# Layer 0 of a four-layer graph kernel: y1 summed on GpSimd before its transposition, and the adjacency's diagonal fetched by strided DMAs

## The chip, the cores and the metric

The kernel runs on one core of one Trainium2 chip. The metric is the device time of one execution in microseconds; a time of several runs is their median. The core has TensorE (PE, with its weight loads shown apart as PEld), VectorE (DVE), ScalarE (ACT), GpSimd (POOL) and SyncE (SP), which here only issues DMAs. All engines run their own instruction queue in order and wait for each other by semaphores.

## The reference, cut to what matters

Four layers follow one another, each of the form `x = layernorm(x + layer(x, adj))`, with x of shape (8, 2048, 64) and adj of shape (2048, 2048). The change is in layer 0:

```python
def _L0_gnn_ref(x, A, embedding, weight, bias):
    K, N = weight.shape[1], A.shape[-2]                      # K = 3, N = 2048
    w = jnp.einsum('nd,dkio->nkio', embedding, weight)
    b = jnp.einsum('nd,do->no', embedding, bias)
    As = [jnp.eye(N, dtype=x.dtype), A]
    As.append(2.0 * (A @ As[-1]) - As[-2])
    x_g = jnp.einsum('knm,bmc->bnkc', jnp.stack(As, 0), x)
    return jnp.einsum('bnki,nkio->bno', x_g, w) + b
```

So layer 0 needs x, y1 = A x and 2 A y1 - x. The matrix A that setup_inputs makes is a 0/1 pattern with each row divided by its sum and with ones on the pattern's diagonal. Row n of A is therefore a 0/1 row times one number, and that number stands on A's diagonal. The kernel calls it s1; it computes with the 0/1 mask and scales the rows of the product by s1.

## The kernel before, in words

Data are held with 128 graph nodes on the partitions and batch and feature (8 x 64 = 512) along the free dimension; there are 16 such node tiles. fp32 values that go through the fast fp32r matmul are split into a rounded part and a remainder (x_hi and x_lo, y_hi and y_lo), and both are multiplied.

**First product** (`first_product`, lines 404 to 508). It makes y1 = s1 * (mask @ x). It runs over four quarters of 512 output nodes, and in each quarter over eight pieces (four blocks of A's transpose, two halves each), 32 pieces in all. `begin(n)`, called two pieces ahead, has SyncE load the piece of A (`raw`, line 439), has VectorE turn it into the 0/1 mask `m` (line 441) and, in the first quarter only, loads a block of x and splits it (`split_x`: load at line 414, x_hi on ScalarE at line 419, x_lo on VectorE at line 420). raw and xraw share four buffers. A piece is sixteen matmuls (line 471) into four accumulator banks, one for each output tile of the quarter; the pool has six banks, and a seventh and eighth belong to small work (`sm0`).

The diagonal is taken in the same pass. In the quarter's first two pieces VectorE multiplies the diagonal blocks with the identity (`dg`, line 451). PE sums them over the partitions by a matmul with ones (`sp`, line 483), ScalarE copies the result into a row `sb` (line 486), one piece later four single-column matmuls turn the row into columns (`sc`, line 491), and VectorE copies them into `s1` (line 495). At the quarter's end ScalarE writes `y_hi` (line 500) and VectorE `y_lo` (line 501), both scaled by s1. After the last quarter the row goes to DRAM as `s_row` (line 507), and `s2 = 2 * s1` is made on VectorE (line 508). Between the pieces runs a generator, `steps`, that prepares membership lists for layer 1 (pT, oh, S, rk; the constants tri, ltri and iota for it are made by GpSimd).

**The loop of layer 0** (`layer0`). For each of the 16 node tiles: SyncE loads two halves of A (`load_adj`, line 966) and the row of s1 for that tile, spread over the partitions (`srow`, line 972), and the x pieces (`load_x`); VectorE makes the mask (`mask`, line 986); GpSimd multiplies the mask by srow and sums its columns (`scaled`, lines 994 to 1002), and VectorE compares that with A (`compare`, line 1007). `first_terms` transposes y1 of the tile for the later matmuls: for each of four 128-column blocks two fp32r matmuls with the identity, one of y_hi and one of y_lo, which PSUM adds up (line 1017); ScalarE copies the result out as y1T (line 1022). `product` makes the second product (line 1044), `second_term` transposes it by `transpose`, a plain fp32 transpose on PE (line 154). `weigh` multiplies the three terms by the weights (line 1081), and VectorE sums them up with the embedding as factor (line 1092). The loop is written as a software pipeline: in iteration j, between the eight groups g of tile j's `weigh`, it runs `scaled(j + 1, 0)` after g = 1, `first_terms(j + 1)` after g = 2, and the product, the comparison and the masks of the next tiles after g = 3.

**What sets the order.** The engines' compute instructions inside `with program_order()` keep the order in which the code calls them, each engine for itself. All else (SyncE's DMAs, and instructions outside those blocks, s2 among them) is placed by a scheduler between them, as early as it reckons that its inputs are there. Buffers come from pools with a fixed number per tag; a tile that takes over a buffer waits for the last reader of the one before. Memory of a pool that is closed is used again by the next, so first tiles of the loop also wait for the last stores of the first product.

Of the kernel before, what the change touches and what calls it, by code (L numbers as in the profile page):

```python
# [8 lines left out]
F32 = mybir.dt.float32  # L9
# [9 lines left out]
P = 128  # L19
# [32 lines left out]
def kernel(  # L52
# [350 lines left out]

    def first_product(own, pre, rawp, mskp, y_hi, y_lo, prepare):

        sb = pre.tile([P, N], F32, tag="sb", name="sb")
        x_hi, x_lo = buffer(own, 0, "x_hi"), buffer(own, 1, "x_lo")
        with tc.tile_pool(name="acc0", bufs=6, space=PSUM) as ps_acc, tc.tile_pool(
            name="sm0", bufs=1, space=PSUM
        ) as ps_s:  # L410
            def split_x(g, h):
                raw = rawp.tile([P, 2, QW], F32, tag="raw", name=f"xraw_{g}_{h}")
                lo = g * QW + h * 2 * P
                nc.sync.dma_start(
                    raw, xn[lo:lo + 2 * P, :].rearrange("(t p) c -> p t c", p=P)
                )
                for t in range(2):
                    j = 4 * g + 2 * h + t
                    nc.scalar.copy(r_(x_hi[:, j, :]), raw[:, t, :])  # L419
                    nc.vector.tensor_tensor(  # L420
                        r_(x_lo[:, j, :]), raw[:, t, :], x_hi[:, j, :], ALU.subtract
                    )

            steps = prepare(ps_s)
            pieces = [
                (q, i, kk, h)
                for q in range(NQ)
                for i, kk in enumerate([q] + [kk for kk in range(4) if kk != q])
                for h in range(2)
            ]  # L430
            m_of, dgs, accs = {}, {}, {}

            def begin(n):

                if n >= len(pieces):
                    return
                q, i, kk, h = pieces[n]
                raw = rawp.tile([P, 2, QW], F32, tag="raw", name=f"raw_{q}_{kk}_{h}")
                nc.sync.dma_start(raw, at[q, kk][:, 2 * h:2 * h + 2, :])
                m = mskp.tile([P, 2, QW], F32, tag="m", name=f"m_{q}_{kk}_{h}")  # L440
                nc.vector.tensor_scalar(r_(m), raw, 0.0, None, op0=ALU.is_gt)
                m_of[n] = m
                if q == 0:
                    split_x(kk, h)
                if i == 0:

                    if h == 0:
                        dgs[q] = pre.tile([P, 4, P], F32, tag="dg", name=f"dg_{q}")
                    for t in range(2):
                        jj = 2 * h + t  # L450
                        nc.vector.tensor_tensor(
                            dgs[q][:, jj, :], raw[:, t, jj * P:(jj + 1) * P], ident, ALU.mult
                        )

            with program_order():
                begin(0)
                begin(1)
                for n, (q, i, kk, h) in enumerate(pieces):
                    begin(n + 2)
                    qc = slice(q * QW, (q + 1) * QW)  # L460
                    if i + h == 0:
                        accs[q] = [
                            ps_acc.tile([P, BC], F32, tag="acc", name=f"y1p_{4 * q + jj}")
                            for jj in range(4)
                        ]
                    m = m_of.pop(n)
                    for t in range(2):
                        mt = 4 * kk + 2 * h + t
                        for jj in range(4):
                            for part in (x_hi, x_lo):  # L470
                                nc.tensor.matmul(  # L471
                                    accs[q][jj],
                                    r_(m[:, t, jj * P:(jj + 1) * P]),
                                    r_(part[:, mt, :]),
                                    start=i + h + t == 0 and part is x_hi,
                                    stop=i == 3 and h + t == 2 and part is x_lo,
                                )
                        if n > 8 or (n, t) == (6, 0):
                            for _ in range(1 + t):
                                next(steps, None)  # L480
                    if (i, h) == (0, 1):
                        sp = ps_s.tile([P, QW], F32, tag="sp", name=f"sp_{q}")
                        nc.tensor.matmul(
                            sp, ones, dgs[q].rearrange("p j n -> p (j n)"), start=True, stop=True
                        )
                        nc.scalar.copy(sb[:, qc], sp)
                    if (i, h) == (1, 0):
                        sp = ps_s.tile([P, QW], F32, tag="sp", name=f"sc_{q}")
                        for jj in range(4):
                            j = 4 * q + jj  # L490
                            nc.tensor.matmul(
                                sp[:, jj:jj + 1], sb[0:1, j * P:(j + 1) * P], ones[0:1, 0:1],
                                start=True, stop=True,
                            )
                        nc.vector.tensor_copy(cols_of["s1"][:, 4 * q:4 * q + 4], sp[:, 0:4])
                    if (i, h) == (3, 1):
                        for jj in range(4):
                            j = 4 * q + jj
                            s = cols_of["s1"][:, j:j + 1]
                            nc.scalar.activation(r_(y_hi[:, j, :]), accs[q][jj], AF.Copy, scale=s)  # L500
                            nc.vector.scalar_tensor_tensor(
                                r_(y_lo[:, j, :]), accs[q][jj], s, y_hi[:, j, :],
                                op0=ALU.mult, op1=ALU.subtract,
                            )
                for _ in steps:
                    pass
            nc.sync.dma_start(s_row, sb[0:1, :])
            nc.vector.tensor_scalar(cols_of["s2"], cols_of["s1"], 2.0, None, op0=ALU.mult)

    @with_exitstack  # L510
# [428 lines left out]
    def layer0(  # L939
# [21 lines left out]
        def load_adj(j):  # L961
            raws[j] = []
            for h in range(2):
# [4 lines left out]
                        at[j // 4, 2 * h + k][:, :, (j % 4) * P:(j % 4 + 1) * P],  # L968
                    )
                raws[j].append(raw)  # L970
            srow[j] = tile("srow", f"srow_{j}", (P, P), 3)
            nc.sync.dma_start(srow[j], s_row[0, j * P:(j + 1) * P].partition_broadcast(P))

        def load_x(j):
# [37 lines left out]
        def first_terms(j):  # L1012

            tr = ps_tr.tile([P, NP, P], F32, tag="tr", name=f"try1_{j}")
            for pr in range(NP):
                for part in (y_hi, y_lo):
                    nc.tensor.matmul(  # L1017
                        tr[:, pr, :], r_(part[:, j, pr * P:(pr + 1) * P]), r_(ident_r),
                        start=part is y_hi, stop=part is y_lo,
                    )  # L1020
            y1T = tile("y1T", f"y1T_{j}", (P, NP, P))
# [1061 lines left out]
```

## Time and profile before

| | |
|---|---|
| median of 3 runs | 1359.8 us (1359.33 to 1364.57) |
| profiled execution | 1364.6 us |
| its span, first to last instruction | 1362.9 us |
| PE busy | 1304.4 us, 96% |
| VectorE busy | 919.2 us, 67% |
| GpSimd busy | 420.2 us, 31% |
| ScalarE busy | 370.7 us, 27% |
| mean granted PE clock | 0.96 |
| first PE matmul | 7.1 us |
| end of the first product's matmuls | 148.7 us |
| layer 0's loop | about 153 to 715 us |

[...]

This is not to be read as PE at its peak, as a matmul counts as busy while it is in the pipeline; PE's time is better read from where its instructions start. "Idle before, releaser" in the other views names the event that ended an engine's waiting. The chain of waits goes back from the last instruction to what released it, again and again; a share in it is time that the end of the span depended on.

### The profile page before, as it was taken

The numbers are of one execution on the slowest core, as the hardware profiler recorded it, in microseconds if no ns is written. First come the engines' busy times: TensorE is split into PE (matmuls) and PEld (weight loads), VectorE is DVE, ScalarE is ACT, GpSimd is POOL, SyncE is SP. The second block draws the span as 40 slices with busy tenths as digits, with TensorE's granted clock in tenths as the row PEclk, the third lists the DMA queues.
The fourth block names the chain that finished last, engine by engine and source line by source line (L and its number), as shares of the span: only waits on it lengthen the run. The fifth ranks groups of instructions, "written<-read, shape, count | busy, mean of one in ns | idle before, by whom it ended". The sixth has DMA issues, their size and how long they took to land.

```text
span 1362.9 us, 20154 instructions
## 1 busy us (share of the span) xinstructions
PE 1304.4 (96%) x7884; PEld 1019.4 (75%) x7884; DVE 919.2 (67%) x1611; ACT 370.7 (27%) x844; POOL 420.2 (31%) x353
## 2 busy tenths in 40 slices
PE   7999899999999999999986799999998899999997
PEld 6777688888888888888874466666665788888885
DVE  4555378787777777777663768888885656666454
ACT  3000101121112222222221345666665521111111
POOL 0000353444444444444210445666553510000000
PEclk9999899999999999999985788999998899999999
DMA  8865432333333333331604111222220223334552
GB/s 285 238 187 167 135 111 89 104 103 103 103 103 103 103 103 104 104 101 55 232 24 140 69 52 65 77 78 78 78 78 1 93 94 124 115 109 141 185 185 72
DMA packets 91047, 153.01 MB, mean 112 GB/s; under 512 B 12097, under 2 KB 55489, under 8 KB 84673
## 3 DMA queue, kind: packets, MB, share of 16 engines
q1 hardware_dynamic: 88642, 147.46, 32.4%
q10 hardware_dynamic: 2304, 4.20, 0.8%
q8 instruction: 64, 1.05, 0.3%
q14 instruction: 37, 0.30, 0.1%
HBM read 115.97 MB, written 35.66 MB: 111 GB/s over the span
## 4 chain that ended last, share of the span: by engine, by line
PE 92%; DVE 3%; ACT 2%; DMA 1%; issue 1%; POOL 0%; SPq 0%; ACTq 0%; DVEq 0%; POOLq 0%
PE pp L1081 25%; PE a L1353 17%; PE ind L1353 9%; PE y2p L1044 9%; PE y1p L471 9%; PE fc L801 3%; PE df L810 2%; PE gp L696 2%; PE trm L154 1%; PE yp L1441 1%; PE try L1017 1%; PE aggp L1190 1%; PE dp L721 1%; PE sgp L1138 1%; PE red L746 1%; PE u L866 1%
## 5 line engine op out<-in xcount | busy, mean ns | idle before, releaser
L1092 DVE SCALAR_TENSOR_TENSOR r<-pp,emb_sb,r 128x256 f32<-128x256 f32 x512 | 247.4, 483 | 123.5 <-PE pp L1081 109.8
L1081 PE MATMUL pp<-w_sb,xT 64*128 64x256 f32 x1024 | 160.4, 390 | 1.7 <-DVE r L1092 1.7
L1081 PE MATMUL pp<-w_sb,y1T 64*128 64x256 f32 x1024 | 153.5, 376 | 0.0
L1081 PE MATMUL pp<-w_sb,y2T 64*128 64x256 f32 x1024 | 153.5, 376 | 0.0
L1030 POOL TENSOR_TENSOR r<-xs,bn 128x256 f32<-128x256 f32 x32 | 22.6, 727 | 413.7 <-issue 263.0
L471 PE MATMUL y1p<-x_hi,m 128*128 128x512 f32 x256 | 106.7, 417 | 7.2 <-ACT x_hi L419 7.1
L1081 PEld LDWEIGHTS pp<-w_sb,xT 64*128 64x128 f32 x1024 | 94.4, 186 | 25.1 <-issue 14.9
L737 POOL TENSOR_TENSOR ez<-ez,coef 128x1024 f32<-128x1024 f32 x32 | 65.1, 2033 | 142.2 <-DVE ez L735 119.8
L1081 PEld LDWEIGHTS pp<-w_sb,y1T 64*128 64x128 f32 x1024 | 99.7, 187 | 10.9
L1081 PEld LDWEIGHTS pp<-w_sb,y2T 64*128 64x128 f32 x1024 | 99.6, 187 | 11.0
L1353 PE MATMUL ind<-y_hi,mj_l 128*128 128x512 f32 x256 | 106.2, 415 | 0.8 <-DVE dlt L766 0.7
L1044 PE MATMUL y2p<-y_hi,msk 128*128 128x512 f32 x256 | 103.7, 405 | 0.0
L471 PE MATMUL y1p<-x_lo,m 128*128 128x512 f32 x256 | 101.9, 398 | 0.0
L1353 PE MATMUL a<-y_hi,mj_l 128*128 128x512 f32 x256 | 101.3, 396 | 0.6 <-ACT y_hi L874 0.6
L1044 PE MATMUL y2p<-y_lo,msk 128*128 128x512 f32 x256 | 101.7, 397 | 0.0
L1353 PE MATMUL a<-y_lo,mj_l 128*128 128x512 f32 x256 | 101.2, 395 | 0.0
L1353 PE MATMUL ind<-y_lo,mj_l 128*128 128x512 f32 x256 | 100.9, 394 | 0.0
L1353 PE MATMUL a<-v_hi,mj_l 128*128 128x512 f32 x256 | 100.1, 392 | 0.0
L1353 PE MATMUL a<-v_lo,mj_l 128*128 128x512 f32 x256 | 99.9, 391 | 0.0
L994 POOL TENSOR_TENSOR ms<-msk,srow 128x1024 f32<-128x1024 f32 x32 | 89.9, 2811 | 5.7 <-DVE ms L1007 5.7
L1353 PEld LDWEIGHTS ind<-y_hi,mj_l 128*128 128x128 f32 x256 | 48.5, 190 | 33.7 <-issue 18.1
L986 DVE TENSOR_SCALAR msk<-adj 128x1024 fp32r<-128x1024 f32 x32 | 63.7, 2024 | 4.1 <-PE y1p L471 4.1
(269 smaller groups left out, 2413.6 us busy)
## 6 DMA issues: line engine op xcount, KB each, us to landing
mj_l<-mask SPq DMA_DIRECT2D x48, 1024.0 KB, 4.9
raw<-in_at SPq DMA_DIRECT2D x32, 512.0 KB, 5.1
adj<-in_at SPq DMA_DIRECT2D x64, 256.0 KB, 3.6
mask<-msk SPq DMA_DIRECT2D x32, 512.0 KB, 4.5
xraw<-in_xn SPq DMA_DIRECT2D x8, 512.0 KB, 5.6
oh<-oh SPq DMA_DIRECT2D x16, 256.0 KB, 3.7
xT<-in_xt SPq DMA_DIRECT2D x16, 256.0 KB, 2.9
xs<-in_xn SPq DMA_DIRECT2D x16, 256.0 KB, 2.8
```

What stands on the lines that cost most here:

```text
L471: nc.tensor.matmul(accs[q][jj], r_(m[:, t, jj * P:(jj + 1) * P]), r_(part[:, mt, :]), start=i + h + t == 0 and part is x_hi, stop=i == 3 a ...
L696: nc.tensor.matmul(gp[:, u, :], r_((oh01, oh23)[i][rs, cols]), r_(part[rs]), start=part is agg_hi, stop=part is agg_lo,)
L737: nc.gpsimd.tensor_tensor(by_b(ez), by_b(ez), per_b(coef, 2 * i, 2), ALU.mult)
L801: nc.tensor.matmul(fc[:, h, :], fcw_sb[rs], sT[rs], start=True, stop=True)
L810: nc.tensor.matmul(df[:, b:b + 1], th[:, b % 2, (b // 2) * P:(b // 2 + 1) * P], av_sb, start=True, stop=True,)
L986: nc.vector.tensor_scalar(r_(m), raws[j][h], 0.0, None, op0=ALU.is_gt)
L994: nc.gpsimd.tensor_tensor(ms, m, srow[j].unsqueeze(1).to_broadcast([P, 8, P]), ALU.mult)
L1030: nc.gpsimd.tensor_tensor(r[:, 4 * bq * C:4 * (bq + 1) * C] .rearrange("p (h l c) -> p h l c", h=2, l=2), swapped(terms[j]["xs"], bq), bn. ...
L1044: nc.tensor.matmul(acc, r_(msk[j, mt // 8][:, mt % 8, :]), r_(part[:, mt, :]), start=mt == 0 and part is y_hi, stop=mt == NT - 1 and part ...
L1081: nc.tensor.matmul(pp[:, h, pl, :], terms[j][name][rs, 2 * bq + pl], w_sb[rs, k, dq * 4 * C:(dq + 1) * 4 * C], start=k == 0, stop=k == K - 1,)
L1092: nc.vector.scalar_tensor_tensor(rb, ppv[:, :, dd, :], emb_sb[:, j, d:d + 1], rb, op0=ALU.mult, op1=ALU.add)
L1353: nc.tensor.matmul(acc, r_(a[:, mt, :]), r_(part[:, mt, :]), start=mt == 0 and part is hi, stop=mt == NT - 1 and part is lo,)
```

## The change

There are three edits.

- In the first product dg, sp, sb, sc and their copies are gone. When piece 7 is begun, GpSimd issues four DMAs (one for each quarter, 128 partitions x 4 elements of 4 bytes, strided in DRAM along the diagonal) straight into s1, and then one DMA that writes s1 from SBUF to s_row. The accumulator pool gets a seventh bank in place of the bank that sp and sc used in turns with the lists' work: sm0 keeps its one bank for the lists.
- In the loop, tiles 2 to 15: GpSimd adds y_hi and y_lo into a tile y1 (one buffer), and PE transposes that by `transpose`, four instructions in place of eight. Tiles 0 and 1 stay as they were.
- srow has two buffers in place of three.

```diff
     def first_product(own, pre, rawp, mskp, y_hi, y_lo, prepare):
-        sb = pre.tile([P, N], F32, tag="sb", name="sb")
         x_hi, x_lo = buffer(own, 0, "x_hi"), buffer(own, 1, "x_lo")
-        with tc.tile_pool(name="acc0", bufs=6, space=PSUM) as ps_acc, tc.tile_pool(
+        with tc.tile_pool(name="acc0", bufs=7, space=PSUM) as ps_acc, tc.tile_pool(
             name="sm0", bufs=1, space=PSUM
         ) as ps_s:
...
-                if i == 0:
-
-                    if h == 0:
-                        dgs[q] = pre.tile([P, 4, P], F32, tag="dg", name=f"dg_{q}")
-                    for t in range(2):
-                        jj = 2 * h + t
-                        nc.vector.tensor_tensor(
-                            dgs[q][:, jj, :], raw[:, t, jj * P:(jj + 1) * P], ident, ALU.mult
+                if n == 7:
+
+                    for qq in range(NQ):
+                        d = at[qq, qq]
+                        nc.gpsimd.dma_start(
+                            cols_of["s1"][:, 4 * qq:4 * qq + 4],
+                            bass.AP(d.tensor, d.offset, [[4 * QW + 1, P], [QW + P, 4]]),
                         )
+                    nc.gpsimd.dma_start(
+                        s_row.rearrange("o (t p) -> p (o t)", p=P), cols_of["s1"]
+                    )
...
-                    if (i, h) == (0, 1):
-                        sp = ps_s.tile([P, QW], F32, tag="sp", name=f"sp_{q}")
-                        nc.tensor.matmul(
-                            sp, ones, dgs[q].rearrange("p j n -> p (j n)"), start=True, stop=True
-                        )
-                        nc.scalar.copy(sb[:, qc], sp)
-                    if (i, h) == (1, 0):
-                        sp = ps_s.tile([P, QW], F32, tag="sp", name=f"sc_{q}")
-                        for jj in range(4):
-                            j = 4 * q + jj
-                            nc.tensor.matmul(
-                                sp[:, jj:jj + 1], sb[0:1, j * P:(j + 1) * P], ones[0:1, 0:1],
-                                start=True, stop=True,
-                            )
-                        nc.vector.tensor_copy(cols_of["s1"][:, 4 * q:4 * q + 4], sp[:, 0:4])
...
-            nc.sync.dma_start(s_row, sb[0:1, :])
             nc.vector.tensor_scalar(cols_of["s2"], cols_of["s1"], 2.0, None, op0=ALU.mult)
...
-            srow[j] = tile("srow", f"srow_{j}", (P, P), 3)
+            srow[j] = tile("srow", f"srow_{j}", (P, P))
...
         def first_terms(j):
             tr = ps_tr.tile([P, NP, P], F32, tag="tr", name=f"try1_{j}")
+            if j > 1:
+                y1 = tile("y1", f"y1_{j}", bufs=1)
+                nc.gpsimd.tensor_tensor(y1, y_hi[:, j, :], y_lo[:, j, :], ALU.add)
             for pr in range(NP):
+                pc = slice(pr * P, (pr + 1) * P)
+                if j > 1:
+                    transpose(tr[:, pr, :], y1[:, pc])
+                    continue
+
                 for part in (y_hi, y_lo):
                     nc.tensor.matmul(
-                        tr[:, pr, :], r_(part[:, j, pr * P:(pr + 1) * P]), r_(ident_r),
+                        tr[:, pr, :], r_(part[:, j, pc]), r_(ident_r),
                         start=part is y_hi, stop=part is y_lo,
                     )
```

More of the change, by code (lines that the diff above doesn't have):

```diff
@@ L430, in first_product @@
             ]
-            m_of, dgs, accs = {}, {}, {}
+            m_of, accs = {}, {}
             def begin(n):
@@ L459, in first_product @@
                     begin(n + 2)
-                    qc = slice(q * QW, (q + 1) * QW)
                     if i + h == 0:
```

## The prediction, made before the changed kernel had run

> **What bounds the kernel now.** I read the page first (span, engines, the chain of waits), then the stretches of the two stages that the change touches, then the chain inside them, and last the time lines of VectorE, GpSimd and SyncE, and what the DMA queues moved.
>
> ```profile
> span 1362.9 us, 20154 instructions
> PE 92%; DVE 3%; ACT 2%; DMA 1%; issue 1%; POOL 0%; SPq 0%; ACTq 0%; DVEq 0%; POOLq 0%
> ```
>
> TensorE holds 92% of the chain that ended last. The stretches say whether that is so where the change is made (the columns are the time, then the busy time of PE, PEld, DVE, ACT and POOL, the granted clock, the DMA share, GB/s):
>
> ```profile
> 20.00:60.00 40.00, 40.00 (x180) 31.91 (x180) 21.87 (x48) 7.87 (x14) 0.00 (x0) 1.00 0.87 251
> 60.00:120.00 60.00, 58.78 (x249) 44.08 (x248) 34.86 (x101) 5.44 (x9) 0.00 (x0) 1.00 0.59 179
> 163.00:715.00 552.00, 547.46 (x4292) 459.92 (x4290) 419.79 (x786) 108.74 (x217) 220.66 (x202) 0.99 0.31 102
> ```
>
> PE is full from 20 us on in the first product and full in the tile loop of layer 0 (163 to 715 us); VectorE there is at 76%, GpSimd at 40%. In the first product the DMA is the runner-up: 87% of its time up to 60 us, 59% after. So a PE instruction taken out of either stage is time, unless something else comes late. The chain gives the prices:
>
> ```profile
> 17.30 0.86 PE sp L483 x2
> ...
> 21.83 0.98 PE sc L491 x8
> ...
> 49.10 1.05 PE sp L483 x2
> ...
> 54.25 0.98 PE sc L491 x8
> ```
>
> ```profile
> 271.89 1.04 PE try L1017 x8
> ...
> 292.91 0.59 PE try L154 x4
> ```
>
> The first pair are the diagonal's two visits to PE, in two of the four quarters. The second set out the two ways of transposing 128x512 in the loop: y1 today, as hi plus lo in eight matmuls (1.04 us), y2 as four plain transposes (0.59 us).
>
> **What the Trainium skill says.** "TensorE: Matmul & The Clock Gate", Part 4, gives about 275 ns for a 128x128 transpose in a kernel; the trace has a median of 273 ns, issued 0.11 us apart. The same page ("Why this matters for your kernels") warns that a gap of over some 3 us drops PE to half clock. The trace agrees: after 148.7 us PE has only 1.7 us of work in 4.6 us, and from 153.3 to 159.0 us its matmuls come 0.43 us apart, not 0.23. "DMA: Bandwidth & Descriptors", "Rules for kernel authors", says that a non-contiguous last dimension lowers to one descriptor per element, and its section "SWDGE vs HWDGE vs iDMA" that DMAs issued by GpSimd have their descriptors written by software on its cores; before has no DMA issued by GpSimd, so no row prices that. "SBUF — State Buffer", "SBUF: two separate sides", adds that such descriptor writing is shut out while VectorE runs a two-port operation; not shown by the trace of before.
>
> **The change part by part.**
>
> *Diagonal off PE.* Removed in each quarter: two matmuls of the ones product and four single-column groups. The chain's eight entries are 0.86 + 1.05 + 1.06 + 0.91 = 3.88 us for sp and 4 x 0.98 = 3.92 us for sc, in all 7.8 us. Of this 5.9 us lies in quarters two to four, where PE is full; 1.84 us lies in the first quarter, where the loads are close behind. VectorE also loses 16 products of 0.285 us (4.6 us), ScalarE four copies of 0.59 us; neither is on the chain, but the products held raw buffers, and SyncE's next loads waited for them 13.3 us in six waits. I count 7.8 us.
>
> *Seventh accumulator bank.* Three instead of two banks are free when a quarter begins. PE waited for y_lo twice, 0.9 us with the weight loads counted. I take 0.3 us.
>
> *y1 by transposes.* Fourteen tiles x (1.04 - 0.59) = 6.3 us. The upper end is 0.44 us per four, as trx shows: 8.4 us. The loop is PE's: VectorE's steps wait for it, not the reverse.
>
> ```profile
> DVE r L1092 <- PE pp L1081: 109.8, 77, 7.4
> ```
>
> *The sum on GpSimd.* Fourteen additions of 128x512; the nearest row is the 128x512 addition of line 998, 1.27 us. It stands in GpSimd's order behind the column sums of the next tile's first half:
>
> ```profile
> 254.29 1.27 POOL L998 TENSOR_TENSOR cs<-msk 128x512 f32<-128x512 f32 x1
> ...
> 256.45 0.46 POOL L1000 TENSOR_TENSOR cs<-cs 128x128 f32<-128x128 f32 x1
> 275.65 1.41 POOL L1030 TENSOR_TENSOR r<-xs,bn 128x256 f32<-128x256 f32 x2 [18.75 <-issue]
> ```
>
> So it can run at 257 to 258.2 us, while PE wants it at 271.9: cover of 13 us, and GpSimd then idles 18.75 us anyway. Cost nothing; behind PE's wait stands the whole tile, so without that cover a delay would be paid in full. Tile 2 is the tightest (column sums done at 190.4, transposed at 204.8) and still has 13 us. One buffer for y1 is enough, since its last reader is a tile back. VectorE's comparison (292.3 us) may meet it for a few tenths; VectorE has idle time behind it.
>
> *Two srow buffers for three.* It looks like a new wait in SyncE's queue, but the queue already waits here:
>
> ```profile
> SPq L972 <- POOL ms L994: 43.0, 13, 6.9
> ```
>
> With three buffers the load runs one tile further ahead and waits for the same GpSimd product that the load of the nearer tile waits for with two. Same place, same releaser; what is loaded (at 212.4 us, say) is next read at 252 us. Nothing.
>
> *The diagonal by DMA.* This is the open price. Four loads of 512 elements of 4 B, then a store of 2048 elements to s_row, all issued by GpSimd. In the built program they are not at the seventh piece: the first load stands before ident is finished, the others directly after it, all before 2 us if issuing were free. The store waits for all four, and behind it stand tri, ltri and iota, which PE first needs at 48.7 us. ScalarE's y_hi needs the data at about 39 us. The early reader is another: VectorE's s2 = 2 s1 (line 507 before) was the last instruction of the stage, and in the built program it is VectorE's eleventh, right after the mask of the third piece, and waits for all four loads. Queued behind it are the x_lo and masks of every later piece, and PE behind those. The time line of before, where that point is:
>
> ```profile
> 13.68 0.69 DVE L441 TENSOR_SCALAR m<-raw 128x1024 fp32r<-128x1024 f32 x1 [1.58 <-DMA raw<-in_at]
> 15.63 1.29 DVE L420 TENSOR_TENSOR x_lo<-xraw,x_hi 128x512 fp32r<-128x512 f32 x2 [1.26 <-ACT x_hi L419]
> ```
>
> PE takes the third piece at 17.0 us without sp, so the loads must have landed by 17.0 - 0.7 (half of x_lo) = 16.3 us. Later costs a microsecond per microsecond, and a gap of several us costs PE 2.7 us more at half clock (13 matmuls x 0.2 us, as at 153 us). For the transfer itself the nearest row is pm, 2048 packets of 256 B:
>
> ```profile
> DMA packets 3707, 3.93 MB, mean 327 GB/s; under 512 B 2341, under 2 KB 2469, under 8 KB 3707
> ```
>
> That is 8 to 20 us; pm landed 7.5 us after its issue beside full-rate loads, so 2048 small packets need at most 7.5 us. In the changed program pm is issued only after the ninth raw load, so the diagonal takes the place that pm had. Descriptor writing is unknown: from below four fixed shares of about 2 us by the DMA page ("Anatomy of one DMA", fit), overlapped or not, so landing at 5 to 10 us; from above I allow 20 ns a descriptor, 2048 x 20 ns = 41 us. I take 12 to 17 us, so no or hardly any stall, because the page calls descriptor generation small. The store's 2048 scattered writes, and pm now among the loads of 30 to 40 us (DMA at 99% there), can push raw loads that have 3 to 5 us in hand: 0 to 4 us, taken 2.
>
> **Sum.** 7.8 + 0.3 + 6.3 - 2.0 = 12.4 us. The profiled execution took 1364.6 us (span 1362.9 and 1.7 around it), so 1352.2; the median of the three runs is 4.8 us lower, so 1347.4 us. The tail of the stage (145 to 153 us, oh store, then srow, et, bp) moves with PE and stays.
>
> **Rivals.**
> - *Loads land at 20 to 28 us.* VectorE stalls 4 to 12 us and PE restarts cold: 14.4 - (24 - 16.3) - 2.7 = 4.0 us left at 24 us, 1355.8 us. For it: no row prices GpSimd's descriptors. Against: pm's transfer is quick, and few two-port operations run on VectorE before 14 us.
> - *Slower.* The same wait, with landing past 28 us, where 14.4 - 11.7 - 2.7 = 0. At 40 us (19 ns a descriptor) the loss is 26.4 us: 1371.8 us. Against it: the page's small share for descriptors.
> - *The loop gains nothing* (the sum comes late or VectorE takes over): 12.4 - 6.3 = 6.1 us, 1353.7 us. Against: 13 us of cover and VectorE's 109.8 us of waiting.
> - *The diagonal costs nothing at all*: 14.4 us, 1345.4 us, or 1343.3 with the upper end of the transposes.
>
> **How the numbers follow.** Likeliest case with its cheap end (1343 to 1351): 0.67. Moderate stall (1351 to 1360): 0.20. Loop gains nothing: 0.04. Slower: 0.09. 0.5% (6.8 us) is about what a measurement here tells from no change; faster by more means below 1353.0: 0.67 + 0.07 of the second case + 0.02 of the third = 0.76. Slower by over 0.5%, above 1366.6: 0.08. Within: 0.16. The range 1343.5 to 1357 leaves out the slower case, the end of the second and a little below.
>
> **What would show it.** Right: no sp or sc on PE; try on the plain transpose at 0.59 us with no wait for GpSimd; a tile period 0.45 us below 34.4; s2 on VectorE starting before 16 us. Wrong: VectorE idle before s2 with a DMA as releaser, PE idle at the third piece and matmuls 0.43 us apart after it; long GpSimd DMA instructions at the start; masks waiting for raw loads between 20 and 45 us.

## The result, and the profile after

The changed kernel takes 1354.49 us (median of 8 runs, 1351.41 to 1355.84), the kernel before 1359.63 us in the same session (8 runs). The medians differ by 5.1 us (0.38%). The ratio estimated from all the runs, which need not equal that of the medians, is 0.9946 with a 95% interval of 0.9923 to 0.9969: faster by 4.2 to 10.5 us. Forecast were 1347.4 us, a gain of 12.4. The profiled execution has a span of 1354.0 us, 8.9 us less than the one of before. The two traces show where those lie. Layer 0 ends 6.0 us earlier (trx is PE's transposition of the layer's result, the last that PE does for it; first before, then after):

```profile
711.77 1.11 PE L154 MATMUL trx<-ident,x 128*128 128x128 f32 x4 [1.29 <-DVE x L1118]
...
705.76 1.11 PE L154 MATMUL trx<-ident,x 128*128 128x128 f32 x4 [2.11 <-DVE x L1110]
```

The other 2.9 us appear in layer 1, whose code is the same in both. I count them as a difference between executions, and use the end of layer 0 as yardstick beside the medians: it is set by the stages that were changed, and nothing of layer 1 is in it. One trace below, that of the diagonal part alone, is of a slow execution (1381.8 us); it is read only up to the end of layer 0, where it agrees with the fast ones.

The stretches that were shown of before (time, busy time of PE, PEld, VectorE, ScalarE, GpSimd, granted clock, DMA share, GB/s) now read:

```profile
20.00:60.00 40.00, 33.18 (x134) 26.03 (x132) 17.53 (x32) 8.12 (x14) 0.00 (x0) 0.91 0.88 261
60.00:120.00 60.00, 59.23 (x249) 44.88 (x248) 34.75 (x93) 4.84 (x8) 0.00 (x0) 1.00 0.66 190
163.00:710.00 547.00, 541.37 (x4239) 453.04 (x4237) 422.33 (x787) 108.01 (x220) 239.58 (x217) 0.99 0.31 103
```

The last two are as full as before. The first is not: from 20 to 60 us PE had been busy all the 40 us at full clock, now it is busy for 33.2 and part of that at a lower clock. So PE work was taken out of a stretch, and more idle time than that came in. When each quarter of the first product ends is read from ScalarE's four y_hi copies of the quarter (start, duration, then in brackets the wait before it). Before:

```profile
40.00 2.42 ACT L500 ACTIVATE y_hi<-y1p,s 128x512 fp32r<-128x512 f32 x4 [6.51 <-PE y1p L471]
...
147.51 2.42 ACT L500 ACTIVATE y_hi<-y1p,s 128x512 fp32r<-128x512 f32 x4 [23.92 <-PE y1p L471]
```

After:

```profile
46.12 2.42 ACT L485 ACTIVATE y_hi<-y1p,s 128x512 fp32r<-128x512 f32 x4 [5.98 <-PE y1p L471]
80.05 2.42 ACT L485 ACTIVATE y_hi<-y1p,s 128x512 fp32r<-128x512 f32 x4 [31.51 <-PE y1p L471]
114.37 2.42 ACT L485 ACTIVATE y_hi<-y1p,s 128x512 fp32r<-128x512 f32 x4 [31.90 <-PE y1p L471]
149.27 2.42 ACT L485 ACTIVATE y_hi<-y1p,s 128x512 fp32r<-128x512 f32 x4 [32.48 <-PE y1p L471]
```

The first quarter ends 6.1 us later than before. From the first y_hi to the fourth it is 103.15 us instead of 107.51, so quarters two to four do gain 4.4 us (forecast were 5.9, and 0.3 for the bank), and the stage as a whole is still 1.8 us late. The stretch from the fourth y_hi to the first weighing of tile 0, called the tail below, makes those up: it takes 15.7 us instead of 17.4, as less of it runs at the lower clock (0.91 against 0.83 from 150 to 170 us). Where tile 0 begins its weighing, both kernels stand at the same time (before, then after):

```profile
164.93 0.70 PE L1081 MATMUL pp<-w_sb,xT 64*128 64x256 f32 x4
...
164.94 0.70 PE L1073 MATMUL pp<-w_sb,xT 64*128 64x256 f32 x4
```

All of the gain is made after that, in the tile loop.

What happens in the first quarter is in GpSimd's time line of the changed kernel (the DMAs are written at piece 7, but stand near the start of the program):

```profile
1.37 1.00 POOL L448 DMA_DIRECT2D s<-in_at  x1 [0.36 <-issue]
...
2.73 2.27 POOL L448 DMA_DIRECT2D s<-in_at  x3
...
10.69 1.17 POOL L452 DMA_DIRECT2D s_row<-s  x1 [4.89 <-DMA s<-in_at]
```

Four loads of 512 elements are issued in 3.3 us, and all have landed when the store of the 2048 elements goes out at 10.69 us. The stretches from there on:

```profile
8.00:12.00 4.00, 4.00 (x13) 3.23 (x13) 2.27 (x5) 1.14 (x2) 1.31 (x2) 1.00 1.06 322
12.00:16.00 4.00, 4.00 (x19) 3.30 (x18) 2.54 (x5) 1.14 (x2) 2.20 (x5) 1.00 1.44 199
16.00:20.00 4.00, 4.00 (x19) 3.22 (x18) 0.70 (x1) 0.00 (x0) 0.00 (x0) 1.00 0.90 44
20.00:24.00 4.00, 0.35 (x2) 0.00 (x0) 0.00 (x0) 0.00 (x0) 0.00 (x0) 1.00 0.60 43
24.00:28.00 4.00, 1.56 (x3) 1.02 (x4) 1.58 (x3) 1.14 (x2) 0.00 (x0) 0.56 0.95 309
```

The last column falls from 322 to 43 GB/s for as long as the store is under way, while the share of time in which the DMA engines are busy stays high (0.90, 0.60): they are shown as occupied and move next to nothing. Who pays is in ScalarE's and PE's time lines:

```profile
25.77 1.14 ACT L418 CAST x_hi<-xraw 128x512 fp32r<-128x512 f32 x2 [11.32 <-DMA xraw<-in_xn]
```

```profile
26.44 0.80 PE L471 MATMUL y1p<-x_hi,m 128*128 128x512 f32 x1 [6.09 <-ACT x_hi L418]
...
28.19 0.63 PE L471 MATMUL y1p<-x_lo,m 128*128 128x512 f32 x1
28.62 0.63 PE L471 MATMUL y1p<-x_hi,m 128*128 128x512 f32 x1
...
31.71 0.40 PE L471 MATMUL y1p<-x_hi,m 128*128 128x512 f32 x1
```

A piece of x that was asked for at 12.5 us arrives at 25.8; PE stands for 6.1 us and then runs at half speed (matmuls 0.43 us apart instead of 0.23) until 31.2 us. That is 6.1 us of standing and 11 matmuls that take 0.2 us longer each, 8.3 us in all.

In the loop the rows of y1 are as forecast. PE's transposes and GpSimd's sum, by tile:

```profile
L154 PE MATMUL try<-ident,y x112: 272/273/330, 204.8 to 666.9; 128*128 128x128 f32 x112
```

```profile
L1001 POOL TENSOR_TENSOR y<-y_hi,y_lo x14: 1290/1296/1307, 190.4 to 631.0; 128x512 f32<-128x512 f32 x14
```

Between the first sum (190.4 us) and the first transpose that reads it (204.8) lie 14 us; nobody waits for the sum.

The theory to be tested is then: *the y1 part gives its 6.3 us in full; the diagonal part gives nothing, because the store of 2048 single elements chokes the loads of the first quarter.* Rivals for the choke are the four strided loads, SyncE's new order (pm, fcw and pT, small loads of lists and weights for layer 1, now issued at 37 to 43 us among the raw loads), and, for the whole, that the y1 part is worth less than it seems.

### The profile page after: what moved, and what is told of

Read it like the earlier page. It is cut to its first block, busy times and chain, and to the rows that moved or that the text cites. A ratio compares the mean times of both kernels' runs of the same rounds, so it can differ in the third digit from the quotient of the medians.

```text
span 1354.0 us, 19969 instructions
## 1 busy us (share of the span) xinstructions
PE 1287.4 (95%) x7788; PEld 1006.0 (74%) x7788; DVE 917.9 (68%) x1591; ACT 367.0 (27%) x840; POOL 443.7 (33%) x372
## 4 chain that ended last, share of the span: by engine, by line
PE 88%; DVE 5%; DMA 3%; ACT 2%; issue 1%; POOL 0%; SPq 0%; ACTq 0%; DVEq 0%; POOLq 0%
PE pp L1073 24%; PE a L1345 17%; PE ind L1345 10%; PE y2p L1036 9%; PE y1p L471 6%; PE fc L785 3%; PE df L794 2%; DMA xraw<-in_xn 2%; PE gp L680 2%; PE aggp L1182 1%; PE try L154 1%; PE trm L154 1%; PE yp L1433 1%; PE sgp L1130 1%; PE red L730 1%
## 5 line engine op out<-in xcount | busy, mean ns | idle before, releaser
L471 PE MATMUL y1p<-x_hi,m 128*128 128x512 f32 x256 | 106.3, 415 | 14.1 <-ACT x_hi L418 13.3
L1073 PEld LDWEIGHTS pp<-w_sb,y1T 64*128 64x128 f32 x1024 | 99.9, 187 | 10.7
L471 PEld LDWEIGHTS y1p<-x_hi,m 128*128 128x128 f32 x256 | 49.5, 194 | 26.9 <-ACT x_hi L418 13.8
```

The costliest lines, as they stand in the source:

```text
L471: nc.tensor.matmul(accs[q][jj], r_(m[:, t, jj * P:(jj + 1) * P]), r_(part[:, mt, :]), start=i + h + t == 0 and part is x_hi, stop=i == 3 a ...
L1073: nc.tensor.matmul(pp[:, h, pl, :], terms[j][name][rs, 2 * bq + pl], w_sb[rs, k, dq * 4 * C:(dq + 1) * 4 * C], start=k == 0, stop=k == K - 1,)
```

## The experiments

Each kernel was compared with the kernel before on the same chip. The table gives the median, the ratio with its 95% interval, and from the trace the start of the first and of the fourth quarter's y_hi and of the last trx of PE, with which layer 0 ends (all in us).

| kernel | median | ratio | first y_hi | fourth y_hi | end of layer 0 |
|---|---|---|---|---|---|
| before | 1359.6 | 1 | 40.0 | 147.5 | 711.8 |
| after | 1354.5 | 0.9946 (0.9923 to 0.9969) | 46.1 | 149.3 | 705.8 |
| y1 part alone | 1354.7 | 0.9964 (0.9942 to 0.9986) | 40.0 | 147.5 | 705.6 |
| diagonal part alone | 1360.0 | 1.0008 (0.9991 to 1.0026) | 45.4 | 148.0 | 712.0 |
| store late | 1358.3 | 0.9984 (0.9972 to 0.9997) | 37.5 | 151.3 | 707.9 |
| row by PE | 1346.2 | 0.9914 (0.9900 to 0.9928) | 38.6 | 141.3 | 697.8 |
| row through SBUF | 1355.7 | 0.9962 (0.9946 to 0.9978) | 44.7 | 148.7 | 706.5 |
| row by PE, pm early | 1350.4 | 0.9920 (0.9901 to 0.9940) | 39.0 | 141.8 | 699.6 |
| store twice | 1362.2 | 1.0014 (0.9996 to 1.0032) | 54.5 | 158.8 | 715.4 |
| wide store | 1347.6 | 0.9898 (0.9874 to 0.9922) | 37.6 | 140.4 | 698.3 |
| far store | 1348.3 | 0.9915 (0.9887 to 0.9944) | 38.4 | 141.9 | 698.3 |
| columns twice | 1347.9 | 0.9903 (0.9865 to 0.9942) | 37.8 | 140.3 | 699.0 |
| six banks | 1347.6 | 0.9901 (0.9872 to 0.9930) | 38.0 | 140.7 | 698.6 |

Ends of layer 0 that should be alike (row by PE, wide store, columns twice, six banks) lie within 1.2 us; differences below that are not read. Most of this spread comes from the tail, which takes 15.6 to 15.8 us in five of the kernels (after, store late, row by PE, store twice, far store) and 17.0 to 17.6 us in the eight others. No run shows what decides between the two, so a gain or loss of some 1.6 us that lies in the tail is not credited to a change here. What the first product gains is better read from the fourth y_hi.

### The two parts apart

The y1 part alone: the kernel before with this part of the change, and two srow buffers.

```diff
+            if j > 1:
+                y1 = tile("y1", f"y1_{j}", bufs=1)
+                nc.gpsimd.tensor_tensor(y1, y_hi[:, j, :], y_lo[:, j, :], ALU.add)
...
+                if j > 1:
+                    transpose(tr[:, pr, :], y1[:, pc])
+                    continue
```

> The kernel before with only the y1 part (sum on GpSimd and plain transposes for tiles 2 to 15) and two srow buffers; the diagonal stays on PE. Theory (the y1 part gives its 6.3 us in full, the diagonal part as a whole gives nothing): 1353.3 us, ratio 0.995; first product as before, first y_hi at 40 us, fourth at 147.5 us. Rival (the 5.1 us gained come from the first product as well, and the y1 part is worth less, say 3 us): 1356.6 us.

The four y_hi are those of before to within 0.05 us, and layer 0 ends 6.15 us earlier, 6.0 of them gained in the loop:

```profile
705.62 1.11 PE L154 MATMUL trx<-ident,x 128*128 128x128 f32 x4 [0.56 <-DVE x L1126]
```

The median is 4.8 us lower, with an interval (1.9 to 7.9 us) that holds both theories' values; it is the trace that decides for the 6.3.

The diagonal part alone: the changed kernel with the y1 part taken back.

```diff
-            if j > 1:
-                y1 = tile("y1", f"y1_{j}", bufs=1)
-                nc.gpsimd.tensor_tensor(y1, y_hi[:, j, :], y_lo[:, j, :], ALU.add)
...
-            srow[j] = tile("srow", f"srow_{j}", (P, P))
+            srow[j] = tile("srow", f"srow_{j}", (P, P), 3)
```

> The changed kernel with the y1 part undone (two matmuls a piece, y_hi and y_lo, as before; three srow buffers); the diagonal by DMA and seven accumulator banks stay. Theory (what the diagonal saves on PE is eaten in the first quarter by the 2048 single stores to s_row): 1359.6 - 5.1 + 6.3 = 1360.8 us, within 2 us of the kernel before; first y_hi at about 46 us, fourth at about 149 us. Rival (the diagonal gains its 7.8 us and the y1 part is worth nothing or hurts): 1351.8 us, first y_hi at 40 us or earlier.

1360.0 us, a ratio of 1.0008, and layer 0 ends at 712.0 us: the diagonal part is worth nothing, within the spread. The gap at 20 us is there as in the changed kernel (first y_hi at 45.4 us). The two parts add up within the spread: 6.15 and -0.2 us, against 6.0 for the whole.

### Is it the store, and does it matter where?

The store late: the same store, from a copy of s1, at the eighteenth piece.

```diff
-                    nc.gpsimd.dma_start(
-                        s_row.rearrange("o (t p) -> p (o t)", p=P), cols_of["s1"]
-                    )
+                if n == 18:
+                    s1c = pre.tile([P, NT], F32, tag="s1c", name="s1c")
+                    nc.scalar.copy(s1c, cols_of["s1"])
+                    nc.gpsimd.dma_start(
+                        s_row.rearrange("o (t p) -> p (o t)", p=P), s1c
+                    )
```

> The changed kernel, but the store of 2048 single elements to s_row is issued at the eighteenth piece (from a copy of s1 made on ScalarE there, at about 75 to 85 us), where the loads run ahead of PE; the four loads of the diagonal and SyncE's order stay as they are. Theory (it is the store in the load-bound first quarter): first y_hi at 38 to 40 us instead of 46, no gap of PE at 20 to 26 us, total 1346 to 1349 us. First rival (the four strided loads of the diagonal choke the DMA): nothing changes, 1354.5 us, first y_hi at 46 us. Second rival (pm, fcw and pT between the raw loads at 37 to 43 us): first y_hi at 43 to 45 us, total about 1352 to 1353 us. Third rival (the store costs the same wherever it stands): the first quarter is quick, but a gap of about 6 us appears after 80 us, total 1354 us.

The first two rivals fall: with the four loads and SyncE's order as they were, the first y_hi is at 37.5 us. But the theory missed on the total, and the third rival is nearer. The choke moved along with the store, which is issued at 73.3 us and lands 13.6 us later:

```profile
80.00:84.00 4.00, 4.00 (x19) 3.05 (x18) 2.00 (x6) 0.00 (x0) 0.00 (x0) 1.00 0.32 18
84.00:88.00 4.00, 4.00 (x19) 3.03 (x18) 1.08 (x3) 0.00 (x0) 0.00 (x0) 1.00 0.62 28
88.00:92.00 4.00, 0.83 (x4) 0.36 (x2) 0.00 (x0) 0.00 (x0) 0.00 (x0) 1.00 0.84 256
92.00:96.00 4.00, 0.00 (x0) 0.00 (x0) 0.00 (x0) 0.00 (x0) 0.00 (x0) 0.53 0.82 258
```

PE is still fed while the DMA is down to 18 to 28 GB/s, as its pieces had been loaded ahead. It stops at 88.8 us, when the DMA is running again. The waits of VectorE and PE say why:

```profile
96.91 0.47 DVE L1328 TENSOR_TENSOR prod<-wb,vecs 64x64 f32<-64x64 f32 x2 [10.98 <-DMA vecs<-in_a_node]
...
98.41 0.29 DVE L397 TENSOR_TENSOR oh<-sm,iota 64x128 fp32r<-64x128 f32 x1
```

```profile
98.76 0.42 PE L374 MATMUL sm<-tri,pT 64*128 64x64 f32 x1 [9.93 <-DVE oh L397]
```

VectorE's order holds a small product of weights (line 1328) here; the weights it reads were asked for only at 88.0 us, behind the choked loads in SyncE's queue, and took 8.9 us to land, and with VectorE stood PE. So a place where the big loads have time in hand was no cover: a 32 KB load that nobody counts as urgent had none. Whether the raw loads alone would have been covered, this run does not tell.

The row by PE: no single-element store at all.

```diff
-                    nc.gpsimd.dma_start(
-                        s_row.rearrange("o (t p) -> p (o t)", p=P), cols_of["s1"]
-                    )
+                if n == 14:
+                    sp = ps_s.tile([P, QW], F32, tag="li", name="s1T")
+                    transpose(sp[0:NT, 0:P], cols_of["s1"])
+                    s1T = pre.tile([NT, P], F32, tag="s1T", name="s1T_sb")
+                    nc.scalar.copy(s1T, sp[0:NT, 0:P])
+                    nc.scalar.dma_start(s_row.rearrange("o (t p) -> (o t) p", p=P), s1T)
```

> The changed kernel without the 2048 single stores: s1 (128x16) is transposed on PE at the twelfth piece to 16x128, copied by ScalarE, and stored to s_row as 16 rows of 512 B from ScalarE's queue. Theory: the same as with the late store or 1 us better, 1345 to 1348 us (one small matmul and one small copy more, at most 1 us on PE), first y_hi at 38 to 40 us. First rival (the four loads): 1354.5 us and first y_hi at 46 us. Second rival (pm, fcw and pT): 1352 to 1353 us, first y_hi at 43 to 45 us.

As the theory says: 1346.2 us, 13.3 below the median of before (by the ratio 9.8 to 13.6), and faster than the changed kernel. The first quarter in this kernel, then the end of layer 0:

```profile
20.00:60.00 40.00, 39.54 (x172) 31.39 (x172) 20.95 (x44) 6.34 (x12) 0.00 (x0) 1.00 0.85 266
```

```profile
697.77 1.12 PE L154 MATMUL trx<-ident,x 128*128 128x128 f32 x4 [2.11 <-DVE x L1113]
```

Against before, layer 0 ends 14.0 us earlier. Of these 6.0 lie in the loop, 1.8 in the tail, which is a short one here, and 6.2 before the fourth y_hi: that is what the diagonal gives without its store. In the six kernels with the row by PE it is 5.6 to 7.2 us. Against the changed kernel, whose tail is as short, the fourth y_hi and the end of layer 0 both come 8.0 us earlier: that is the price of the store (7.4 to 9.0 by the fourth y_hi of the six). The four strided loads are still in this kernel, and cost nothing that shows.

### SyncE's order, and the seventh bank

pm early: the row by PE, with the loads of pm, fcw, fcb and pT asked for before the piece loop.

```diff
                 begin(1)
+                next(steps, None)
                 for n, (q, i, kk, h) in enumerate(pieces):
...
-                        if n > 8 or (n, t) == (6, 0):
+                        if n > 8:
```

> The row made on PE, and the loads of pm, fcw, fcb and the first pT_raw issued after the second piece, as early as in the kernel before, instead of after the ninth. Theory (SyncE's new order costs nothing once the single stores are gone): within 1.5 us of the row made on PE (1346 us), first y_hi at 38 to 40 us. Rival (the late pm holds up raw loads at 37 to 43 us): 1 to 2 us better, 1344 to 1345 us. Other way: 0.77 MB more among the first loads, which are what the first quarter waits for, costs up to 2.6 us at about 295 GB/s: 1348 us.

No gain: the first and the fourth y_hi are 0.4 us later, and layer 0 ends 1.8 us later than with the row by PE, but 1.4 of these lie in the tail. The median of 1350.4 us lies above all three expectations (six runs, 1347.5 to 1353.0), while the intervals of the ratios overlap. The rival that the late pm costs 1 to 2 us falls; whether the early one costs up to 2 us stays open.

Six banks: the row by PE with `bufs=6` for acc0.

```diff
-        with tc.tile_pool(name="acc0", bufs=7, space=PSUM) as ps_acc, tc.tile_pool(
+        with tc.tile_pool(name="acc0", bufs=6, space=PSUM) as ps_acc, tc.tile_pool(
```

> The row made on PE with six accumulator banks instead of seven in the first product. Prediction's term: the seventh bank is worth 0.3 us, so PE waits for y_lo two or three times, 0.5 us in all, and the total is that of the row made on PE plus 0.3 us, within its interval (1346 to 1348 us). Rival (the bank was worth 2 us or more): the quarters two to four are 0.5 us longer each, fourth y_hi 2 us later.

The wait that the prediction had read in before comes back with six banks: between 30 and 150 us PE's weight loads wait twice for y_lo, and with seven banks they do not.

```profile
PEld y1p L474 <- DVE y_lo L489: 0.9, 2, 0.5
```

But no matmul of the product waits for y_lo, and from the first y_hi to the fourth it is 102.7 us with six banks and 102.8 with seven. Layer 0 ends 0.9 us later, inside the spread, and this lies in the tail. So the bank is worth nothing that shows.

### What about the store is expensive?

A second store of the same kind, directly behind the first:

```diff
+                    nc.gpsimd.dma_start(
+                        s_again.rearrange("o (t p) -> p (o t)", p=P), cols_of["s1"]
+                    )
```

> The changed kernel with a second store of the same 2048 single elements to another row in DRAM that nobody reads, directly behind the first. Theory (the price is that of the single writes and goes by their number): another 8 to 12 us in the first quarter, first y_hi at 54 to 58 us, total 1363 to 1367 us. Rival (the price is a fixed one of having such a store, or was not the store at all): 1354 to 1356 us, first y_hi at 46 to 47 us.

The first y_hi goes from 46.1 to 54.5 us and the end of layer 0 from 705.8 to 715.4: 8.4 to 9.7 us for the second store, about as much as for the first (8.0). The median of 1362.2 us is 0.8 below what was expected; the price is not a fixed one.

So far "many single elements" would do as an explanation. Four kernels, all with the row by PE or through SBUF, change what is stored or loaded at this place. The first has the row loaded a second time by single elements, into one partition of SBUF, and stored from there in one piece:

```diff
+                        nc.gpsimd.dma_start(
+                            sb[:, qq * QW:(qq + 1) * QW],
+                            bass.AP(d.tensor, d.offset, [[0, 1], [QW + P, 4], [4 * QW + 1, P]]),
+                        )
...
+                    nc.sync.dma_start(s_row, sb)
```

> The changed kernel without the 2048 single stores: GpSimd loads the diagonal twice, as columns into s1 and as a row into one partition of SBUF (four more loads of 512 elements of 4 B), and SyncE stores the row to s_row as one piece of 8 KB. Theory (single-element writes to DRAM are what chokes; single-element reads from it are not): as with the row made on PE, 1345 to 1348 us, first y_hi at 38 to 41 us (twice the loads may land some us later and hold up s2). Rival (any few thousand packets of 4 B choke the DMA; now 4096 reads instead of 2048 reads and 2048 writes): 1354 us or more, first y_hi at 46 us or later, DMA under 100 GB/s somewhere between 3 and 25 us.

Here my theory was wrong: 1355.7 us, first y_hi at 44.7, and between 8 and 20 us the DMA moves 115, 127 and 54 GB/s. Without any single write to DRAM the choke is back. The columns twice: the same number of single reads, but the second four also spread over 128 partitions (nobody reads them).

```diff
+                        nc.gpsimd.dma_start(
+                            s1b[:, 4 * qq:4 * qq + 4],
+                            bass.AP(d.tensor, d.offset, [[4 * QW + 1, P], [QW + P, 4]]),
+                        )
```

> The row made on PE, and the four loads of the diagonal's columns issued twice, the second time into a tile that nobody reads: 4096 single elements read from DRAM, written over 128 partitions. It differs from the kernel that lost (columns and row by single reads, 1355.7 us) only in that the second four go to 128 partitions and not into one. Theory (not the reads, but many single writes into one row): DMA stays above 280 GB/s between 8 and 20 us, first y_hi at 38 to 41 us, 1346 to 1348 us. Rival (the number of single-element reads: 2048 fit, 4096 do not): first y_hi at 44 us or later, 1352 to 1356 us.

No choke, first y_hi at 37.8 us. So 4096 single reads alone do not choke. That it is the destination, though, this pair does not show cleanly. By the code both kernels load 4096 elements, 16 KB, but what GpSimd's DMA queue moved in the whole execution (packets, MB, share) differs, first the row through SBUF, then the columns twice:

```profile
q0 software_dynamic: 320, 0.04, 0.4%
...
q0 software_dynamic: 256, 0.02, 0.1%
```

The loads into one partition moved more than they were asked for, and they also read the diagonal in another order. Which of the three counts, one partition, more traffic or the order, no run separates. The far store: 2048 single writes to DRAM from the same tile, at the same point of GpSimd's order, but each at least 512 B from the next, over 1 MB in place of 8 KB (besides the row by PE; nobody reads them).

```diff
+                    nc.gpsimd.dma_start(
+                        s_far.rearrange("(t p) c -> p t c", p=P)[:, :, 0:1],
+                        cols_of["s1"].unsqueeze(2),
+                    )
```

> The row made on PE, and besides a store of the 2048 elements of s1 one by one, where the changed kernel stores s_row, but each to a row of its own in DRAM (512 B from one to the next, read by nobody), so that the destinations do not lie side by side. Theory (the price goes with the number of single-element writes, wherever they go): as in the changed kernel, the store lands after 12 to 16 us, DMA under 100 GB/s from 16 to 24 us, first y_hi at 44 to 47 us, total 1346 + 8 = 1354 us. Rival (the price comes from writes side by side in one small region, as in s_row and in the row in one partition): lands in 3 to 7 us, first y_hi at 38 to 40 us, total 1346 to 1347 us.

The wide store: the same 8 KB in 128 pieces of 64 B.

```diff
+                    nc.gpsimd.dma_start(s_wide, cols_of["s1"])
```

> The row made on PE (s_row stored as 16 rows of 512 B), and besides a store of s1 to a place in DRAM that nobody reads, issued by GpSimd where the changed kernel stores s_row, but with 64 B in one piece from each partition: 128 pieces instead of 2048 of the same 8 KB. Theory (the price goes by the number of pieces): 128/2048 of some 8 us is 0.5 us; the store lands in 2 to 4 us, first y_hi at 38 to 40 us, total as the row made on PE, 1346 to 1347 us. Rival (any store issued by GpSimd into this stretch, or any 8 KB in pieces under 512 B, chokes the loads): first y_hi at 44 us or later, 1351 us or more.

The DMA view of the stretch from 10 to 26 us sets them side by side: what was moved, and for each group of transfers, the size in KB and the median us from issue to landing. The changed kernel:

```profile
DMA packets 1018, 2.36 MB, mean 148 GB/s; under 512 B 130, under 2 KB 194, under 8 KB 1018
...
xraw<-in_xn SPq DMA_DIRECT2D x2, 512.0 KB, 13.4
...
s_row<-s POOLq DMA_DIRECT2D x1, 8.0 KB, 13.8
```

The store twice:

```profile
DMA packets 792, 1.70 MB, mean 106 GB/s; under 512 B 121, under 2 KB 185, under 8 KB 792
...
s_row<-s POOLq DMA_DIRECT2D x1, 8.0 KB, 15.5
s_again<-s POOLq DMA_DIRECT2D x1, 8.0 KB, 24.3
```

The row through SBUF:

```profile
DMA packets 1347, 2.81 MB, mean 175 GB/s; under 512 B 319, under 2 KB 383, under 8 KB 1347
...
sb<-in_at POOLq DMA_DIRECT2D x1, 2.0 KB, 12.8
```

The columns twice:

```profile
DMA packets 2311, 5.51 MB, mean 344 GB/s; under 512 B 271, under 2 KB 335, under 8 KB 2311
```

The far store:

```profile
DMA packets 1836, 4.41 MB, mean 276 GB/s; under 512 B 193, under 2 KB 257, under 8 KB 1836
...
s_far<-s POOLq DMA_DIRECT2D x1, 8.0 KB, 6.7
```

The wide store:

```profile
DMA packets 2289, 5.58 MB, mean 349 GB/s; under 512 B 205, under 2 KB 285, under 8 KB 2289
...
s_wide<-s POOLq DMA_DIRECT2D x1, 8.0 KB, 3.7
```

The mean is the thing to read: 344 to 353 GB/s with no single writes close together (353 with the row by PE alone), 276 with 2048 far ones, 148 with 2048 packed into 8 KB, 106 with twice that, 175 with the loads into one partition. The far store still costs: it lands in 6.7 us against 3.7 for the wide one, holds the DMA at 181 GB/s from 16 to 20 us, and moves the first y_hi by less than 1 us. GpSimd's queue shows the same 176 packets and 0.02 MB for the far store as for the packed one of the changed kernel, so these two stores differ in the destination alone. So for stores to DRAM two things matter: the number of single-element writes, and how closely their destinations lie together; only with both was the first quarter held up. The Trainium skill, "DMA: Bandwidth & Descriptors", section "Specifications", says that below 512 B the DMA does a read-modify-write. Packed single elements would then share such units and have to take turns, which fits the stores; but no run here shows the inside of the transfer, and 64 B pieces, which are below 512 B too, show no loss. A rival fits as well: 1 MB may be spread over more of the memory than 8 KB. Neither was tested, so the reason stays open.

## Why the prediction was right and where it failed

The range (1343.5 to 1357) and the sign held; the time was 7.1 us off, and most of that comes from one term. That the range held is in part luck: its upper half was there for loads that land late, and these were not late.

- *Diagonal off PE*, 7.8 us: right in kind, somewhat too large. With the store out of the way 5.6 to 7.2 us are gained by the fourth y_hi; quarters two to four, where 5.9 were forecast, gain 4.4 in the changed kernel and 4.8 with the row by PE. Why not all of it shows was not tested. *Seventh accumulator bank*, 0.3 us: the waits are there as read, but taking the bank back costs nothing that shows.
- *y1 by transposes*, 6.3 us: right. 6.15 us measured by the part alone, 6.0 of them in the loop; the price of one transposition came out as forecast (eight matmuls became four, each at the 273 ns of before). *The sum on GpSimd* and *Two srow buffers for three* at nothing: right, nobody waits for the sum, and SyncE's wait for GpSimd before srow stays (46.4 us in 14 waits against 43.0 in 13).
- *The diagonal by DMA*, the loads: forecast to land at 12 to 17 us, they landed by 10.7, and VectorE's s2 ran at 13.04 us without a stall. The wait on which I had built two rivals ("loads land at 20 to 28 us" and the slower case) did not happen. GpSimd's issue took 1.0 us for the first load, 0.75 for each other.
- The step that failed, in the prediction's words: "The store's 2048 scattered writes, and pm now among the loads of 30 to 40 us (DMA at 99% there), can push raw loads that have 3 to 5 us in hand: 0 to 4 us, taken 2." Of its two halves, pm costs nothing that shows, and the store costs 8.0 us, twice the upper end. 12.4 with 8.0 in place of 2.0 is 6.4 us, and layer 0 ended 6.0 earlier; that the two are so close is luck again, as the tail, which the prediction held fixed, gave 1.8 us where the diagonal gave less than forecast. The bound was wrong for two reasons. It has no working of its own: the only price of small pieces was pm's, 2048 pieces of 256 B, which are read from DRAM and written over 128 partitions, while the store writes 4 B pieces packed into 8 KB, and how these lie turned out to be the price. And I looked for trouble at 30 to 40 us, though I had the point at which the store would go out: it waits for nothing but the four loads, so it ran at 10.7 us, in the stretch in which every load is waited for.
- *The half clock.* The prediction lets the trace of before agree with a drop after gaps of some 3 us by adding gaps up. No single gap there is that long: the longest between 148.7 and 153.3 us is 2.2 us, and PE's matmuls still come 0.43 us apart afterwards. So the drop is shown, the 3 us are not; the changed kernel's gap of 6.1 us leaves them open too.

The total alone would have misled. 1354.5 us is next to what two of the rivals give (1355.8 for late loads, 1353.7 for a loop that gains nothing), and neither is what happened: s2 did not wait, and the loop gained everything while the first product gained nothing.

The row by PE keeps both parts of the change and gives the store back: 1346.2 us, between the forecast and the case in which the diagonal costs nothing (1345.4); as the diagonal's gain is smaller than in that case, a part of this closeness is chance.

## What to carry to other kernels

Price a DMA by its destination as well as its source: thousands of single elements read from strided places and spread over partitions were nearly free, while the same number written close together in DRAM slowed the core's other transfers for some ten microseconds. A small transfer is not charged to its own waiters but to whoever loads next to it, so ask what the DMA is doing at the moment at which its last input is ready; moving it to one quieter place did not help, turning the tile on PE and storing it in rows did. When a change has two parts, take each alone: here one gave all and the other nothing, which the total hid. And see where in the trace a gain lies: a stretch whose work had not been changed made up 1.8 us.

## What the runs showed of the hardware that was not expected

- A store of 2048 elements of 4 B into 8 KB of DRAM took 13.6 to 15.5 us to land and held the core's DMA at 43 to 44 GB/s for about 8 us, with the DMA engines shown as busy for 60 to 90% of the time (8 to 28 GB/s for some 12 us in the late one, where they are shown as busy for 11 to 62%); two in a row cost twice as much. The same number of elements over 1 MB landed in 6.7 us, the same bytes in 64 B pieces in 3.7 us.
- Four loads of 512 single elements into one partition took 9.6 to 12.8 us to land and came with a choke (54 GB/s from 16 to 20 us), though more bytes were moved than asked for; into 128 partitions such loads land in 6.1 us, also beside other loads at 320 GB/s.
- GpSimd was occupied for only 1.17 us when it issued 2048 single-element writes, and 0.56 us for the 128 wide ones: the time on the issuing engine did not show what the transfer cost.
